# Layer 1's table split by batch, its preparation overlapped with gathers, and layer 2's mixing weights computed in layer 0

## The chip, the cores and the metric

The program runs on one core of one Trainium2 chip, in one launch. The core has five engines that run side by side and are held together by semaphores: PE (matrix multiply), DVE (vector), ACT (scalar), POOL (GpSimd) and SP, which here only issues DMAs. DMAs are issued from SP's queue or from POOL's, and share 16 DMA engines. The metric is the device time of one execution, in microseconds (us).

## The reference

Four layers on x of shape (2, 64, 64, 128): two batches of 4096 tokens with 128 channels. Layer 0 adds a selective scan, layer 1 a deformable convolution, layers 2 and 3 attention-like and feed-forward parts. The change touches layer 1, the beginning of layer 0, and a small preparation for layer 2. Layer 1, on the group-normed x:

```python
offsets = conv3x3(x, offset_w) + offset_b            # 18 = 9 taps x (dy, dx)
py = row + ky + dy;  px = col + kx + dx
y0, x0 = floor(py), floor(px);  wy, wx = py - y0, px - x0
val = gather(y0, x0)     * (1-wy)*(1-wx) + gather(y0, x0+1)     * (1-wy)*wx \
    + gather(y0+1, x0)   * wy*(1-wx)     + gather(y0+1, x0+1)   * wy*wx      # 0 outside the image
out = einsum('bhwkc,kcf->bhwf', val, kernel) + bias
x = x + out
```

Layer 2's feed-forward part mixes four sets of spectral filter matrices with weights from a softmax; the mixed matrices depend on weights alone, not on x:

```python
w = y_hard - y_soft + y_soft          # 4 weights
s = sigma ** 0.25                     # 16 filters
# for each of 4 segments: sums of w[i] * s[f] * (M_phi_plus[i, f] +- M_phi_minus[i, f]), and of w[i] * M_u[i]
```

## The kernel before

The kernel is written in a tile framework: the code lists instructions, and the framework orders them on each engine by a schedule of its own, places tiles in pools, and adds the waits. Pools lie on a stack: a pool that is opened after another has been closed takes its memory. Only inside `manual_schedule` (layer 0's scan loop and layer 2) is the order that of the code. X, the tokens of both batches (64 tiles of 128 tokens x 128 channels), stays on chip through layers 0 and 1.

The stages, in the order of the code (L1356 to L1400):

- X is loaded in 8 DMAs on SP (L1353). `zero_table` (L430) writes zeros over the whole table of layer 1 in DRAM with one DMA from POOL's queue (L437). The table has, for each batch, 67 x 67 cells of 4 x 128 floats (2 KB): cell (y, x) holds the four neighbours that bilinear sampling at that place needs.
- Layer 0 (L159). For each batch: transposes of X to channels (L95), group norm (L126: statistics, two small matmuls with `gmat`, then one pass over `xt`, L146), the gate `z` (L209 to L212, stored to DRAM from SP), the input projection (L221) and the depthwise convolution as 144 matmuls (L227), whose outputs ACT turns into U (L228). Then the scan over 32 chunks (L243 to L395; its first POOL instruction is L281), then the output part (L400 to L425). U and Y are tiles of a pool that lives through both batches (L189, L190).
- Layer 1 (L440), in two stages with pools of their own. Preparation, for batch 0 and then batch 1: transposes, group norm, a copy into the padded image `xp` (POOL, L466), transposes back into `xk` (L472), eight DMAs on SP that write `xk` into the table, shifted four ways (L480), the offset convolution as 72 matmuls with 18 weight columns each (L486; a float32 matmul leaves two records), transposes of the offsets (L491). After both batches: the index and weight arithmetic on DVE, for all 64 tiles at once (L507 to L524), into `idx` and `wt`. Then the loop over 64 tiles: nine gathers on POOL's queue (L534, 128 rows of 2 KB each) into G (three buffers), one multiplication on DVE into V (L541, two buffers), 36 matmuls against the identity that add the four corners and transpose (L553), three copies on ACT (L554), nine matmuls with the kernel (L557), one that adds the bias (L558), and an addition to X on DVE (L559).
- `mixing_weights` (L582) opens its pools before layer 1's, and `work()` is called after layer 1, so that its instructions run beside it: a few small operations, then for each of 16 filters two loads (L646, L647), arithmetic on DVE (L635, L637, L650, L652, L653) and a store (L654).
- `norm_tokens` (L564) takes the statistics of each of the 64 tiles of X (L571, L572), then `rs` and `sh` (L574), which layer 2's first normalisation reads (L729). X is stored to DRAM (L1387 by way of L1353).
- Layers 2 and 3, which the change does not touch.

Of the kernel before, what the change touches and what calls it, by code (L numbers as in the profile page):

```python
# [16 lines left out]
F32 = mybir.dt.float32  # L17
# [141 lines left out]
def layer0(k):  # L159
# [3 lines left out]
    with ExitStack() as es:  # L163
# [26 lines left out]
        Y = big.tile([P, 2, L], F32, name="Y")  # L190
        zs = dr.tile([2, P, B * L], F32, name="zs")

        for b in range(B):
            Xb = X[:, b * NTB : (b + 1) * NTB, :]
            with ExitStack() as e2:
# [20 lines left out]
                for h in range(2):  # L216
# [6 lines left out]
                    for q in range(8):  # L223
                        pc = ps.tile([P, N], F32, name="pc", tag="ps")
                        for t in range(9):
                            ky, kx = divmod(t, 3)
                            nc.tensor.matmul(pc, dw[:, h * 9 + t, :], xp[:, 8 * q + ky : 8 * q + ky + 8, kx : kx + WW], start=t == 0, stop=t == 8)  # L227
                        nc.scalar.activation(U[:, h, q * N : (q + 1) * N], pc, AF.Silu, bias=k.v("conv_b")[:, h : h + 1])  # L228

# [167 lines left out]
            with ExitStack() as e2:  # L397
                wk = e2.enter_context(tc.tile_pool(name=f"l0f{b}", bufs=2))
                ps = e2.enter_context(tc.tile_pool(name=f"l0fs{b}", bufs=6, space=PSUM))
                for q in range(8):  # L400
# [24 lines left out]
                    nc.vector.tensor_tensor(o, po.rearrange("p (a c) -> p a c", c=C), o, ALU.add)  # L425

# [3 lines left out]
def zero_table(k, pool, table):  # L430

    nc = k.nc
    row = B * TS * 4
    z = pool.tile([P, row], F32, name="zero")
    nc.gpsimd.memset(z, 0.0)
    flat = table.rearrange("a c -> (a c)").rearrange("(p g f) -> p g f", p=P, f=row)
    nc.gpsimd.dma_start(out=flat, in_=z.unsqueeze(1).to_broadcast([P, TS, row]))  # L437


def layer1(k, table):  # L440
    tc, nc, ins, X = k.tc, k.nc, k.ins, k.X
    with ExitStack() as es:
        enter = es.enter_context
        cst = enter(tc.tile_pool(name="l1c", bufs=1))
        wt = cst.tile([P, NT * 9, 4], F32, name="wt")
        idx = cst.tile([P, NT * 9], I32, name="idx")
        w_k = cst.tile([P, 9, C], F32, name="w_k")
        nc.sync.dma_start(out=w_k, in_=ins["kern1"].rearrange("t c f -> c t f"))

        with ExitStack() as e2:  # L450
            pre = e2.enter_context(tc.tile_pool(name="l1p", bufs=1))
            ps = e2.enter_context(tc.tile_pool(name="l1ps", bufs=6, space=PSUM))
            gmat = pre.tile([P, P], F32, name="gmat1")
            nc.sync.dma_start(out=gmat, in_=ins["gmat"])
            w_o = pre.tile([P, 9, 18], F32, name="w_o")
            nc.sync.dma_start(out=w_o, in_=ins["offw1"].rearrange("t c f -> c t f"))
            base = pre.tile([P, 2, NT, 9], F32, name="base")
            nc.sync.dma_start(out=base, in_=ins["base"])
            off = pre.tile([P, NT, 18], F32, name="off")
            for b in range(B):  # L460
                xt = pre.tile([P, L], F32, name="xt1")
                to_channels(k, ps, xt, lambda i: X[:, b * NTB + i, :], NTB)
                xp = pre.tile([P, 66, 66], F32, name="xp1", bufs=2)
                zero_frame(nc, xp)
                groupnorm(k, pre, ps, gmat, xt, "gn1")
                nc.gpsimd.tensor_copy(xp[:, 1:65, 1:65], xt.rearrange("p (h w) -> p h w", w=WW))  # L466

                xk = pre.tile([P, NTB, C], F32, name="xk")
                for g in range(0, NTB, 4):
                    pt = ps.tile([P, N], F32, name="pt1", tag="ps")  # L470
                    for j in range(4):
                        nc.tensor.transpose(pt[:, j * P : (j + 1) * P], xt[:, (g + j) * P : (g + j + 1) * P], k.ident)  # L472
                    k.copy(xk[:, g : g + 4, :].rearrange("p a c -> p (a c)"), pt)
                cells = table[b * TS * TS : (b + 1) * TS * TS, :].rearrange("(y x) c -> y x c", x=TS)
                for j in range(4):
                    dy, dx = divmod(j, 2)
                    for yy in range(2):
                        y0 = 2 - dy + yy
                        dst = cells[y0 : y0 + 63 : 2, 2 - dx : 66 - dx, j * C : (j + 1) * C]
                        nc.sync.dma_start(out=dst.rearrange("t x c -> x t c"), in_=xk[64 * yy : 64 * yy + 64, :, :])  # L480
                ot = pre.tile([18, L], F32, name="ot1")
                for q in range(8):
                    po = ps.tile([P, N], F32, name="po1", tag="ps")
                    for t in range(9):
                        ky, kx = divmod(t, 3)
                        nc.tensor.matmul(po[:18, :], w_o[:, t, :], xp[:, 8 * q + ky : 8 * q + ky + 8, kx : kx + WW], start=t == 0, stop=t == 8)  # L486
                    k.copy(ot[:, q * N : (q + 1) * N], po[:18, :])
                for g in range(0, NTB, 16):
                    pt = ps.tile([P, N], F32, name="pt2", tag="ps")
                    for j in range(16):  # L490
                        nc.tensor.transpose(pt[:, j * 18 : (j + 1) * 18], ot[:, (g + j) * P : (g + j + 1) * P], k.ident[:18, :18])  # L491
                    nc.vector.tensor_tensor(
                        off[:, b * NTB + g : b * NTB + g + 16, :],
                        pt[:, : 16 * 18].rearrange("p (a o) -> p a o", o=18),
                        k.r("offset_b").unsqueeze(1).to_broadcast([P, 16, 18]),
                        ALU.add,
                    )

            cell = pre.tile([P, 2, NT, 9], F32, name="cell")
            frac = pre.tile([P, 2, NT, 9], F32, name="frac")  # L500
            rest = pre.tile([P, 2, NT, 9], F32, name="rest")
            pt = pre.tile([P, NT, 9], F32, name="point")
            ti = pre.tile([P, NT, 9], I32, name="ti")
            tf = pre.tile([P, NT, 9], F32, name="tf")
# [11 lines left out]
            for b in range(B):  # L516
                s = slice(b * NTB, (b + 1) * NTB)
                nc.vector.tensor_scalar(cell[:, 0, s], cell[:, 0, s], float(TS), float((b * TS + 2) * TS + 2), ALU.mult, ALU.add)
            nc.vector.tensor_tensor(tf, cell[:, 0], cell[:, 1], ALU.add)
            nc.vector.tensor_copy(idx, tf.rearrange("p t o -> p (t o)"))  # L520
            for j in range(4):
                wy = (frac if j // 2 else rest)[:, 0]
                wx = (frac if j % 2 else rest)[:, 1]
                nc.vector.tensor_tensor(wt[:, :, j], wy.rearrange("p t o -> p (t o)"), wx.rearrange("p t o -> p (t o)"), ALU.mult)  # L524

        with ExitStack() as e2:
            gp = e2.enter_context(tc.tile_pool(name="l1g", bufs=3))
            wk = e2.enter_context(tc.tile_pool(name="l1w", bufs=2))
            ps = e2.enter_context(tc.tile_pool(name="l1gs", bufs=6, space=PSUM))
            po_ = e2.enter_context(tc.tile_pool(name="l1go", bufs=2, space=PSUM))  # L530
            for t in range(NT):
                G = gp.tile([P, 9, 4 * C], F32, name="G")
                for o in range(9):
                    nc.gpsimd.indirect_dma_start(  # L534
                        out=G[:, o, :],
                        out_offset=None,
                        in_=table,
                        in_offset=bass.IndirectOffsetOnAxis(ap=idx[:, t * 9 + o : t * 9 + o + 1], axis=0),
                    )
                V = wk.tile([P, 36, C], F32, name="V")  # L540
                nc.vector.tensor_tensor(  # L541
                    V,
                    G.rearrange("p o (q c) -> p (o q) c", c=C),
                    wt[:, t * 9 : (t + 1) * 9, :].rearrange("p o q -> p (o q)").unsqueeze(2).to_broadcast([P, 36, C]),
                    ALU.mult,
                )

                vt = wk.tile([P, 9 * P], F32, name="vt")
                for g, n in ((0, 4), (4, 4), (8, 1)):
                    pv = ps.tile([P, N], F32, name="pv1", tag="ps")  # L550
                    for o in range(n):
                        for q in range(4):
                            nc.tensor.matmul(pv[:, o * P : (o + 1) * P], V[:, (g + o) * 4 + q, :], k.ident, start=q == 0, stop=q == 3)  # L553
                    nc.scalar.copy(vt[:, g * P : (g + n) * P], pv[:, : n * P])  # L554
                po = po_.tile([P, C], F32, name="po2")
                for o in range(9):
                    nc.tensor.matmul(po, vt[:, o * P : (o + 1) * P], w_k[:, o, :], start=o == 0, stop=False)  # L557
# [18 lines left out]

DW = 257


def mixing_weights(k, dr, es):  # L582

# [918 lines left out]
```

## Time and profile before

| | us |
|---|---|
| median of 3 runs | 16111.0 |
| the runs | 16098.64 to 16113.83 |
| the profiled execution | 16122.4 |
| its span, from the first to the last instruction | 16120.6 |

Where the edits fall, in the profiled execution, in us from the span's start:

| stage | from | to |
|---|---|---|
| X loaded, table zeroed | 1.7 | 60 |
| layer 0, batch 0, up to the first POOL instruction of the scan (L281) | 60 | 227.66 |
| layer 0, the rest | 227.66 | 4673 |
| layer 1, preparation | 4673 | 4873.77 |
| layer 1, gathers, first start to last end | 4873.77 | 5851.14 |
| last V, last matmuls, statistics (to the start of L729) | 5853.98 | 5873.06 |
| layers 2 and 3 | 5873 | 16120.6 |

An engine's row in the profile gives the line of code, the operation, the tiles written and read, and the duration; text in brackets is how long the engine was idle before it, and what ended that. The granted clock is the share of full speed that PE's clock was given. DMA shares are means over the 16 DMA engines.

### The profile page before, as it was taken

How to read it: one execution, taken by the hardware profiler on the slowest of the kernel's cores; microseconds unless marked ns; L12 is line 12 of the kernel's file. 1: busy time of each engine (PE TensorE's matmuls, PEld its weight loads, DVE VectorE, ACT ScalarE, POOL GpSimd, SP SyncE). 2: the span in 40 equal slices, each digit the busy share in tenths (PEclk: the TensorE clock that was granted, in tenths of full speed). 3: DMA queues.
4: the chain of work that ended last, by engine and by line, in shares of the span. 5: the costliest groups of instructions: out<-in, count | busy, mean ns of one | idle time of the engine just before them, and what ended most of it. 6: DMA issues, size and time to landing. Idle time of an engine off the chain costs nothing.

```text
span 16120.6 us, 190989 instructions
## 1 busy us (share of the span) xinstructions
PE 12236.8 (76%) x69886; PEld 7246.4 (45%) x69886; DVE 13783.2 (86%) x12003; ACT 9835.0 (61%) x15912; POOL 13463.0 (84%) x5125
## 2 busy tenths in 40 slices
PE   6666657666667864549778679879788888888897
PEld 2222223222227851325445446546445555555565
DVE  4999975999964359999999999999999999999973
ACT  3666634666610027777777677777777777777752
POOL 3888835888817879999999999999999999999970
PEclk8999989999988876769889889989999999999998
DMA  2111111111135544546555556556666665565543
GB/s 102 69 71 69 68 51 49 70 71 69 69 93 160 160 143 151 168 150 203 183 187 195 174 181 199 193 184 203 192 193 198 189 204 195 190 205 194 188 169 128
DMA packets 1214859, 2389.69 MB, mean 148 GB/s; under 512 B 346648, under 2 KB 923288, under 8 KB 1047904
## 3 DMA queue, kind: packets, MB, share of 16 engines
q1 hardware_dynamic: 1162672, 2206.74, 41.7%
q0 software_dynamic: 50384, 169.42, 3.5%
q8 instruction: 552, 9.04, 0.2%
q14 instruction: 387, 3.17, 0.1%
q10 hardware_dynamic: 864, 1.32, 0.0%
HBM read 2018.49 MB, written 358.65 MB: 147 GB/s over the span
## 4 chain that ended last, share of the span: by engine, by line
POOL 34%; PE 13%; DVE 10%; DMA 3%; ACT 2%; issue 1%; SPq 0%; POOLq 0%; ACTq 0%; DVEq 0%
POOL S L1082 33%; DVE S L1138 10%; PE pef L966 6%; PE Z L1100 2%; PE acc L939 2%; DMA row<-drow 2%; PE pw L765 1%; POOL S L1088 1%; ACT ze L1106 1%; ACT dA L1136 0%; DMA w<-in_w_b_dram 0%; DMA w<-in_w_delta_dram 0%; ACT e L946 0%; PE acc L1001 0%; DMA e<-mdr 0%
## 5 line engine op out<-in xcount | busy, mean ns | idle before, releaser
L1138 DVE TENSOR_TENSOR_SCAN S<-dA,S 128x512 f32<-128x512 f32 x8192 | 9226.5, 1200 | 393.0 <-ACT dA L1136 208.4
L1082 POOL TENSOR_TENSOR S<-row,g 128x4096 f32<-128x4096 f32 x1024 | 9103.0, 8895 | 256.3 <-DMA row<-drow 219.8
L1136 ACT ACTIVATE dA<-row,a_t 128x512 f32<-128x512 f32 x8192 | 5614.4, 692 | 2146.0 <-DVE S L1138 2107.7
L1100 PE MATMUL Z<-S,cv 128*32 128x256 f32 x32768 | 2499.4, 435 | 1494.0 <-ACT ze L1106 1240.3
L966 PE MATMUL pef<-hk,ur 128*128 128x256 f32 x14336 | 3512.1, 388 | 138.8 <-ACT e L946 120.0
L966 PEld LDWEIGHTS pef<-hk,ur 128*128 128x128 f32 x14336 | 2644.6, 191 | 1077.6 <-issue 563.4
L365 DVE TENSOR_TENSOR_SCAN S<-dA,S 128x1024 f32<-128x1024 f32 x1024 | 2339.1, 2284 | 243.7 <-ACT dA L363 96.8
L354 POOL TENSOR_TENSOR S<-du,br 128x1024 f32<-128x1024 f32 x1024 | 2410.3, 2357 | 138.6 <-DVE M L379 83.3
L1100 PEld LDWEIGHTS Z<-S,cv 128*32 128x32 f32 x32768 | 999.9, 121 | 2698.6 <-issue 1289.2
L394 PE MATMUL yp<-M,ident 128*128 128x512 f32 x4096 | 2062.6, 627 | 2.9 <-DVE M L379 2.9
L394 PEld LDWEIGHTS yp<-M,ident 128*128 128x128 f32 x4096 | 821.7, 201 | 2091.7 <-issue 2052.7
L363 ACT ACTIVATE dA<-dt,an 128x511 f32<-128x511 f32 x2048 | 1406.9, 687 | 209.0 <-DVE S L365 132.0
L379 DVE TENSOR_TENSOR M<-S,pcn 128x1024 f32<-128x1024 f32 x1024 | 1250.5, 1221 | 110.5 <-DVE S L365 6.9
L323 PE MATMUL pcn<-cs,sel 80*128 80x512 bf16 x1024 | 409.3, 400 | 1180.4 <-DVE M L379 1169.8
L1106 ACT COPY ze<-Z 128x512 f32<-128x512 f32 x1024 | 1122.4, 1096 | 235.0 <-PE Z L1100 201.2
L939 PE MATMUL acc<-e,mw 128*128 128x512 f32 x1920 | 1042.2, 631 | 29.1 <-ACT e L946 28.5
L534 POOL DMA_INDIRECT G<-table,idx x576 | 802.2, 1393 | 261.1 <-issue 175.1
L966 PEld LDWEIGHTS pef<-hd,ur 128*128 128x128 f32 x4096 | 761.4, 195 | 491.7 <-issue 233.0
L966 PE MATMUL pef<-hd,ur 128*128 128x256 f32 (+1 forms) x4096 | 882.0, 342 | 99.8 <-ACT e L946 93.8
L541 DVE TENSOR_TENSOR V<-G,wt 128x4608 f32<-128x4608 f32 x64 | 317.5, 4962 | 609.0 <-DMA G<-table,idx 590.9
L367 ACT COPY stt<-S 128x2 f32<-128x2 f32 x896 | 168.9, 189 | 1083.5 <-DVE S L365 1080.3
L553 PE MATMUL pv<-ident,V 128*128 128x128 f32 x4608 | 615.3, 302 | 52.1 <-issue 48.8
(323 smaller groups left out, 8302.1 us busy)
## 6 DMA issues: line engine op xcount, KB each, us to landing
row<-drow SPq DMA_DIRECT2D x1024, 1024.0 KB
br<-bc SPq DMA_DIRECT2D x256, 1024.0 KB
zd<-ze SPq DMA_DIRECT2D x1024, 256.0 KB
hk<-in_phi_dram SPq DMA_DIRECT2D x128, 576.5 KB
hk<-in_phi_dram SPq DMA_DIRECT2D x96, 704.5 KB
hd<-in_phi_dram SPq DMA_DIRECT2D x512, 128.5 KB
mw<-wdr SPq DMA_DIRECT2D x480, 128.0 KB
hk<-in_phi_dram SPq DMA_DIRECT2D x160, 320.5 KB
```

The source lines that it names most:

```text
L354: nc.gpsimd.tensor_tensor(S, du, br[:, n % 4, :].unsqueeze(1).to_broadcast([P, 2, T]), ALU.mult)
L363: nc.scalar.activation(dA[:, h, rest], dt[:, h, rest], AF.Exp, scale=an[:, kk * 2 + h, n : n + 1])
L365: nc.vector.tensor_tensor_scan(flat, dflat, flat, 0.0, ALU.mult, ALU.add)
L379: nc.vector.tensor_tensor(M, S, pcn.unsqueeze(1).to_broadcast([P, 2, T]), ALU.mult)
L394: nc.tensor.matmul(yp[:, h, :], k.ident, M[:, h, :], start=False, stop=n == 15)
L939: nc.tensor.matmul(acc.rearrange("p a s -> p (a s)"), ms[f][:, o, :], e, start=box["first"], stop="whole" in box and (f, o) == todo[-1])
L966: nc.tensor.matmul(pe[:, a, 256 - n :], ur[:, par, j, :], h[:, at : at + n], start=i == 0, stop=i + 1 == len(mm))
L1082: nc.gpsimd.tensor_tensor(S, row.unsqueeze(1).to_broadcast([P, 2, R, T]), g.unsqueeze(2).to_broadcast([P, 2, R, T]), ALU.mult)
L1100: nc.tensor.matmul(Z[32 * j : 32 * j + 32, q], cv[:, h, s], S[:, h, :, s], start=h == 0, stop=h == 1)
L1106: nc.scalar.copy(ze.rearrange("p q t e -> p q e t"), Z)
L1136: nc.scalar.activation(dA, row[:, j % R, :], AF.Exp, scale=a_t[:, h, d : d + 1])
L1138: nc.vector.tensor_tensor_scan(s, dA, s, 0.0, ALU.mult, ALU.add)
```

## The change

Four things are done, in layer 0, layer 1 and the zeroing of the table:

- The table becomes two tables, one for each batch, and only the cells at the border are zeroed (two double rows at top and bottom, and a strip of four cells across each row's end), in six DMAs on POOL's queue.
- Layer 1 has one set of pools. Each batch has its own `idx` and `wt`, and its own index arithmetic, at half the width. The loop of gathers over all 64 tiles follows. Its preparation pool has one buffer a tile. G has four buffers, and V is written in place in G. The copy to `xp` is made on ACT. The bias is added to X ahead of the loop, on DVE, for a whole batch at once, and its matmul is left out.
- The offset convolution has weights padded to 32 columns; four matmuls, for four row groups of the image, write to four column groups of PE and four partition groups of one PSUM tile, so that two such tiles hold a batch's offsets. They are turned back with four full transposes each.
- `mixing_weights` is split into its DRAM tiles and `work(es)`, and layer 0 calls `work` at the end of batch 0's preparation, with pools inside that stage's. Y moves to a pool of its own for each batch, opened after that stage.

```diff
-def layer0(k):
+def layer0(k, mix=None):
...
-        Y = big.tile([P, 2, L], F32, name="Y")
...
+                if b == 0 and mix is not None:
+                    mix(e2)
+
+            yb = es.enter_context(ExitStack())
+            Y = yb.enter_context(tc.tile_pool(name=f"l0y{b}", bufs=1)).tile([P, 2, L], F32, name="Y")
...
+            yb.close()
...
 def zero_table(k, pool, table):
-    row = B * TS * 4
-    z = pool.tile([P, row], F32, name="zero")
+    z = pool.tile([P, 4 * 4 * C], F32, name="zero")
     nc.gpsimd.memset(z, 0.0)
-    flat = table.rearrange("a c -> (a c)").rearrange("(p g f) -> p g f", p=P, f=row)
-    nc.gpsimd.dma_start(out=flat, in_=z.unsqueeze(1).to_broadcast([P, TS, row]))
+    cell = 4 * C
+    for b in range(B):
+        flat = table[b].rearrange("a c -> (a c)")
+        for y in (0, TS - 2):
+            rows = flat[y * TS * cell : (y + 2) * TS * cell].rearrange("(p f) -> p f", p=P)
+            nc.gpsimd.dma_start(out=rows, in_=z[:, : 2 * TS * cell // P])
+        edge = flat[(TS + TS - 2) * cell :]
+        dst = bass.AP(edge.tensor, edge.offset, [[TS * cell, TS - 3], [1, 4 * cell]])
+        nc.gpsimd.dma_start(out=dst, in_=z[: TS - 3, :])
...
 def layer1(k, table):
...
+        pre = enter(tc.tile_pool(name="l1p", bufs=1))
+        gp = enter(tc.tile_pool(name="l1g", bufs=4))
+        wk = enter(tc.tile_pool(name="l1w", bufs=2))
+        ps = enter(tc.tile_pool(name="l1ps", bufs=3, space=PSUM))
+        gs = enter(tc.tile_pool(name="l1gs", bufs=3, space=PSUM))
+        po_ = enter(tc.tile_pool(name="l1go", bufs=2, space=PSUM))
...
+        w_o = cst.tile([P, 9, 32], F32, name="w_o")
+        nc.vector.memset(w_o, 0.0)
+        nc.sync.dma_start(out=w_o[:, :, :18], in_=ins["offw1"].rearrange("t c f -> c t f"))
+        wts, idxs = [], []
+        for b in range(B):
...
+            nc.vector.tensor_tensor(Xb, Xb, k.r("bias1").unsqueeze(1).to_broadcast([P, NTB, C]), ALU.add)
...
-                nc.gpsimd.tensor_copy(xp[:, 1:65, 1:65], xt.rearrange("p (h w) -> p h w", w=WW))
+            nc.scalar.copy(xp[:, 1:65, 1:65], xt.rearrange("p (h w) -> p h w", w=WW))
...
+            for g in range(2):
+                po = ps.tile([P, N], F32, name="po1", tag="ps")
+                for t in range(9):
+                    ky, kx = divmod(t, 3)
                     for j in range(4):
-                        nc.tensor.matmul(po[:18, :], w_o[:, t, :], xp[:, 8 * q + ky : 8 * q + ky + 8, kx : kx + WW], start=t == 0, stop=t == 8)
-                    k.copy(ot[:, q * N : (q + 1) * N], po[:18, :])
...
+                        q = 4 * g + j
+                        nc.tensor.matmul(po[32 * j : 32 * j + 32, :], w_o[:, t, :], xp[:, 8 * q + ky : 8 * q + ky + 8, kx : kx + WW], start=t == 0, stop=t == 8)
+                ot = pre.tile([P, N], F32, name="ot1", bufs=2)
+                k.copy(ot, po)
...
+            idx = cst.tile([P, NTB * 9], I32, name=f"idx{b}")
...
+        for t in range(NT):
+            b, i = divmod(t, NTB)
...
+                    in_=table[b],
...
+            V = G.rearrange("p o (q c) -> p (o q) c", c=C)
+            nc.vector.tensor_tensor(V, V, wts[b][:, i * 9 : (i + 1) * 9, :].rearrange("p o q -> p (o q)").unsqueeze(2).to_broadcast([P, 36, C]), ALU.mult)
...
-                nc.tensor.matmul(po, k.ones, k.r("bias1")[0:1, :], start=False, stop=True)
...
-def mixing_weights(k, dr, es):
+def mixing_weights(k, dr):
...
+    def work(es):
+        cst = es.enter_context(tc.tile_pool(name="f2c", bufs=1))
+        wp = es.enter_context(tc.tile_pool(name="f2w", bufs=2))
...
-                    table = dr.tile([B * TS * TS, 4 * C], F32, name="table")
+                    table = [dr.tile([TS * TS, 4 * C], F32, name=f"table{b}") for b in range(B)]
...
+                    weights, mix = mixing_weights(k, dr)
                 if "0" in stages:
-                    layer0(k)
...
+                    layer0(k, mix)
...
+                if "1" in stages:
+                    layer1(k, table)
...
```

## The prediction

> **What bounds the kernel now.** I read the page first, then the busy time by stretches, then the timeline of the two stages that the edits touch, then the waits. The groups of the page put most of the time into layer 2 (scan L1138 on DVE, inputs L1082 on POOL), which no edit touches. What can move is layer 0 up to its scan and layer 1, which runs from 4673 to 5873 us.
>
> The stretches show two plain bounds. Columns: stretch, its length, busy time of PE, weight loads, DVE, ACT, POOL, then granted clock, share of the DMA engines, GB/s.
>
> ```profile
> 45.00:50.00 5.00, 0.00 (x0) 0.00 (x0) 0.00 (x0) 0.00 (x0) 0.00 (x0) 0.50 1.04 413
> 100.00:150.00 50.00, 50.00 (x118) 22.08 (x117) 0.00 (x0) 4.81 (x7) 0.00 (x0) 1.00 0.00 0
> 4725.00:4730.00 5.00, 5.00 (x13) 1.17 (x12) 0.00 (x0) 0.07 (x1) 0.00 (x0) 1.00 1.00 219
> 5420.00:5470.00 50.00, 44.17 (x336) 42.49 (x336) 16.91 (x12) 4.61 (x10) 40.56 (x31) 0.90 0.57 162
> ```
>
> At 45 us every engine is idle and the DMA engines are full: the table's zeros. From 100 us layer 0's convolution fills PE while DMA and DVE do nothing. At 4725 us PE (offset convolution, L486) and DMA (table writes, L480) are both full. In the gathers nothing is full, though POOL comes near. The timeline there (start, length, engine, line) says why:
>
> ```profile
> 5397.24 4.96 DVE L541 TENSOR_TENSOR V<-G,wt 128x4608 f32<-128x4608 f32 x1 [10.72 <-DMA G<-table,idx]
> 5398.24 4.79 POOL L534 DMA_INDIRECT G<-table,idx  x1 [0.30 <-issue]
> 5402.12 0.28 DVE L559 TENSOR_TENSOR X<-po,X 128x128 f32<-128x128 f32 x1
> 5402.44 0.29 DVE L571 BATCH_NORM_STATS2 st<-X 128x6 f32<-128x128 f32 x1
> 5402.77 0.18 DVE L572 BATCH_NORM_AGGREGATE mv<-st 128x2 f32<-128x6 f32 x1
> 5403.34 0.95 POOL L534 DMA_INDIRECT G<-table,idx  x1 [0.30 <-issue]
> ```
>
> Eight gathers of a tile take 0.96 us each, 0.30 apart. The one caught by DVE's run takes 4.79 and ends 0.08 us after L572, the last operation of that run (5402.95 to 5403.03). I checked all 64 tiles: each has one long gather, and from the fourth on it ends 0.08 or 0.09 after L572. So POOL sets the pace: 9 x 1.26 + 3.8 = 15.1 us a tile, and 977.4 us from the first gather (4873.77) to the end of the last (5851.14). V waits for gathers 590.9 of its 609.0 idle us; PE has slack (12.7 of 15.1).
>
> The waits give the two ends of the stages:
>
> ```profile
> PE pm L136 <- DMA gmat<-in_gmat_dram: 25.5, 1, 25.5
> DVE ot L72 <- PE po L486: 79.4, 6, 14.8
> ACT rt L625 <- PE po L423: 12.2, 1, 12.2
> ```
>
> Layer 0's group norm waits 25.5 us for a 64 KB matrix that is queued behind the zeros. Layer 1's offsets wait for the convolution. The third line I use for memory: `rt` is 64 bytes at the bottom of the new pools, and it waited for the last matmul of layer 0, not for the tile that had lain there: a pool's memory comes free when the pools before it are done.
>
> **Zeros in border cells.** Before: 18.4 MB (17,956 KB, L437). After: per batch two double rows of 2 x 67 x 2 KB and 64 x 8 KB, 1.06 MB; 2.1 MB in all. 16.3 MB less at 413 GB/s = 39.4 us by which gmat, and everything behind it up to the scan, comes earlier (the sum pm starts at 62.97 now). Bounds: 35 (X's 4.2 MB, in rows of 512 bytes, at the 294 GB/s that like loads reach at 4680 us) to 43 (gmat right behind X). I take **-39**. Six short POOL issues take the place of one of 3.2 us; POOL is idle there until 227 us.
>
> **Mixing weights in layer 0.** All of L602 to L654 moves: 16 rounds of L635 0.344, three L637 of 0.478, L650 0.746, L652 0.684, L653 0.682 = 3.89 us, 62 us of DVE; 32 loads and 16 stores on SP, with mu and mdr 18.3 MB: 62 us at 294 GB/s, 85 at the 216 of the table writes. What hides it is the convolution L227, 92 to 223 us, with DVE busy 2.8 us of 100 and DMA at zero. Started behind gmat at about 24 us it ends near 150; the scan would start at about 185 (223 less 39). It is queued on SP among the 16 zs stores (L212, 16.9 us); z waits for these ten times already, 3.1 us in all, and behind z stand PSUM and PE. Bounds 0 to 17 (that stretch doubled); I take **+6**, nearer the 3.1. Two table loads on ACT (1.28 each) fall where ACT idles. If the cover were gone see the rivals. Y, now below the scan's pools, is first written after the convolution either way: 0.
>
> **Batch 0's preparation.** Now the first gather waits for both batches: two convolutions of 62 us one after the other (288 records, 123.9 us busy), and the index work at double width. After, it needs only table 0 and idx 0. Table: writes start at 4700.65 now. The bias add on X (128x4096, 4.96 x 4096/4608 = 4.4 us) comes ahead of part of the group norm; the mix's operations between its steps go, 1.5 us; the copy to xp goes from POOL (3.9 us) to ACT, by its rows 8 x 0.59 = 4.7 at most, ahead of ACT's half of the xk copies, some 3 us. So xk is full at about 4706; 8.4 MB at 218 GB/s = 38.5 us; landed at 4745, gathers from 4747. Offsets: four column tiles side by side. Z at L1100 is the like: 2499.4 us for 32,768 records of 256 columns, 76 ns each, against 123.9/288/2 = 215 for L486. So 144 records of 512 columns take 22 us, not 62; with copies, transposes and index work at half width (8 us) idx 0 is there near 4735, before the table. DVE's queue may hold batch 1's xk copies, which wait for xk to be written out, ahead of idx 0: up to 15 us. I take half of that doubt, gathers from 4752: **-122**. Bounds: -130, and -101 if the column tiles run one at a time (idx at 4772).
>
> **The loop.** Batch 1's 8 MB of table writes and its PE and DVE work now lie beside batch 0's gathers. DMA: 8.4 MB ask for 38 us of full engines beside a loop that uses 0.55, some 85 us of crowding; four G buffers hold 60 us of issue against a life of about 40 (issue 15, landing 3, V 5, PE 13), so landings may slip 20 us before POOL feels it: 0. PE: two times 32 transposes and 22 us more against 2.4 us of slack a tile: absorbed in a dozen tiles. DVE: xt and xk copies 5.5, bias 4.4, statistics 5.0, small ones 1.6, normalising 2.4, offsets 1.6, index work 8: 28.5 us, each of which holds a gather up. Bounds 0 to 29; about half runs before 4752, I take **+12**. G now lives until PE has read it, the in-place V takes as long as before.
>
> L571 and L572 leave the loop: their pool now lies where w_k is, and so waits for the last po. Each tile's DVE run ends 0.55 earlier (5402.40 for 5402.95): 63 x 0.55 = **-35**, with POOL at 14.7 us a tile and PE at 12.
>
> [...] Here the rows show the end of the gather after L572 in 61 tiles, and I go by them.
>
> **The tail.** The same 64 pairs come after the last po: 0.42 us from a pair's start to the next operation (5859.18 to 5859.60), 63 x 0.42 = 26.5 us, ahead of sh (L574) and of layer 2's first xn (L729, released by sh at 5873.06). The bias matmuls (L558) go: 0.8 us of this. **+26**. Bounds 0 (the pool lies elsewhere; then the 35 are not gained either) to 32.
>
> **Sum.** -39 + 6 - 122 + 12 - 35 + 26 = -152. The profiled execution took 16122.4 us (span 16120.6), so 15970; it lay 11 above the runs' median of 16111.0, so the forecast is **15,960 us**. Layers 2 and 3 are unchanged; the runs spread over 15 us.
>
> **Rivals.** (a) The mix keeps its old pace: 4676.65 to 4917 is 240 us; from 24 it would end at 264, and the scan's pools, which take its memory, wait 79 us for it: less the 6, 16,033. For: the release shown by `rt`, two buffers a round, an SP queue that waits. Against: the old pace came from 16 MB of table writes and a busy DVE. 12%.
> (b) The start is held: column tiles one at a time, idx 0 behind batch 1's work, PE 40 us late once more: 21 + 25 more, 16,006. 13%.
> (c) The change doesn't overlap: something of batch 1 (POOL's frame, DVE's order) stands before batch 0's gathers, which then start when table 1 is written, near 4795: 43 - 12 more, 15,991. 7%.
> (d) Slower: the mix is queued behind the convolution, whose outputs end at 184, and runs for its 240 us before the scan: 240 - 6 more, 16,194. It decides from an end of the mix later than about 184 + 158 + 32 = 374 us. For: it is called after the convolution. Against: it was called last before as well, and its first load left 4 us after layer 1 began. 8%.
> My case has 60%.
>
> **How the numbers follow.** My own case reaches from 15,915 (all best bounds: -43, -130, -35, +26, less spread) to 16,000. With (b), (c) and most of (a), and the costs at their upper ends together, I give 15,910 to 16,045. About 0.2% (32 us) is what a measurement here can tell from no change; below 16,079 lie my case, (b), (c) and most of (a): 87%. Within: 5%. Above: 8%.
>
> **What would show it.** pm at 22 to 28 us, the scan's first POOL operation (L281, now 227.66) near 195; the last wdr store before that. First gather 4752 less about 33, long gathers near 4.2 us, ending after the X add; 64 bn pairs in a row after the last po; L1's column tiles overlapping as L1100 does. Wrong if wdr stores run up to the scan's start, if gathers wait for buffers, or if POOL's long gathers multiply in batch 0's half by more than 29 us in sum.

## The result, and the profile after

The changed kernel takes **15,975.8 us** (median of 4 runs, 15,964.0 to 15,978.7); the kernel before, run beside it, 16,112.4 (4 runs, 16,098.6 to 16,122.8). The ratio is 0.9914, with a 95% interval from 0.9897 to 0.9932: some 137 us or 0.9% less. The profiled execution has a span of 15,975.1 us, for 16,120.6 before: 145.5 us less. Cut at the same events in both traces, these go as follows (us; the columns "before" and "after" are times between the two events).

| stretch | before | after | measured | forecast |
|---|---|---|---|---|
| start to group norm's first product, pm | 62.97 | 25.24 | -37.7 | -39 |
| pm to the first z product, pz | 6.2 | 16.9 | +10.7 | +6 for the mix in layer 0 |
| pz to the scan's first POOL operation (L281, now L285) | 158.5 | 159.0 | +0.5 | in the same +6 |
| rest of layer 0 | | | -2.2 | 0 |
| start of layer 1 to the first gather | 200.9 | 72.9 | -128.0 | -122 |
| first gather to the end of the last | 977.4 | 969.3 | -8.1 | +12 - 35 = -23 |
| last gather to layer 2's first xn | 21.9 | 44.9 | +23.0 | +26 |
| layers 2 and 3 | 10247.5 | 10243.9 | -3.6 | 0 |
| sum | | | -145.5 | -152 |

The size of the whole is as forecast; two of its terms are not: the loop's, and the time between pm and the scan. Both are seen in the timeline (start, length, engine, line, operation, and in brackets the idle time before it and what ended it). The rows set at 0, layers 2 and 3 and the rest of layer 0, move by as much between profiles of code that is the same there: layers 2 and 3 take 10,238.7 to 10,249.3 us in seven profiles of the changed kernel and its variants, and from the scan's first POOL operation to the first gather it is 4511.5 to 4517.4 us in seven.

Layer 0's start, kernel after:

```profile
25.24 0.56 PE L136 MATMUL pm<-gn_mv,gmat 128*128 128x1 f32 x2 [7.22 <-DMA gmat<-in_gmat_dram]
...
30.05 0.42 DVE L649 TENSOR_SCALAR mus<-mu,w 128x384 f32<-128x384 f32 x1 [2.17 <-DMA mu<-in_mu_dram]
...
32.26 3.65 DVE L177 CAST sel<-ident 16x2048 bf16<-16x2048 f32 x3
...
37.63 0.15 DVE L84 TENSOR_TENSOR gn_s<-gn_rs 128x1 f32<-128x1 f32 x1
...
42.12 8.05 PE L208 MATMUL pz<-xt,w_in 128*128 128x512 f32 x12 [14.63 <-DVE xt L146]
```

The zeros' part came as forecast: pm waits for gmat until 25.2. But between two small steps of the same group norm DVE now waits for mu, the mix's first load (L649), and then makes layer 0's constants (L175 to L187, 6.4 us); before, those ran at 92 to 99 us, beside the convolution. L84 could have run at about 30.5 and runs at 37.6, and xt, which the products of z wait for, is late with it.

The start of layer 1, kernel after (SPq is SP's DMA queue; the length of the table writes is that of their issue):

```profile
4650.94 4.42 DVE L479 TENSOR_TENSOR X<-X,rv 128x4096 f32<-128x4096 f32 x1
...
4671.09 7.93 PE L506 MATMUL po<-xp,w_o 128*32 128x512 f32 x72
...
4671.81 35.97 SPq L497 DMA_DIRECT2D table<-xk  x8
...
4705.75 0.29 DVE L541 CAST idx<-tf 128x288 int32<-128x288 f32 x1
4716.97 1.07 POOL L554 DMA_INDIRECT G<-table,idx  x1 [27.92 <-DMA base<-in_base_dram]
```

The column-tiled convolution of a batch is two such rows of 72 products, 15.9 us for the 62 before. The index table idx is ready at 4706.0, the first gather starts at 4717.0: the table comes last, as forecast. (The row names the load of `base` for batch 1, which stands on SP's queue right behind the table's eight writes. In a later profile of the same kernel the last write lands at 4710.43, `base` at 4711.19, and the first gather starts at 4711.40, so some 0.8 us of the wait are that load's.)

The loop, kernel after, the same stretch of a tile that the prediction showed of before:

```profile
4808.77 4.96 DVE L561 TENSOR_TENSOR G<-G,wt 128x4608 f32<-128x4608 f32 x1 [9.73 <-issue]
4809.97 4.58 POOL L554 DMA_INDIRECT G<-table,idx  x1 [0.30 <-issue]
4813.65 0.28 DVE L573 TENSOR_TENSOR X<-po,X 128x128 f32<-128x128 f32 x1
4814.86 0.94 POOL L554 DMA_INDIRECT G<-table,idx  x1 [0.30 <-issue]
```

L585 and L586 (L571 and L572 before) have left the loop, and yet the long gather is no shorter: 4.87 us on average (63 of them) for 4.86. It ends at 4814.55, 0.82 us after V's end (4813.73). All 63 do, within 0.01, and read again so do those of before: V at 5397.24 + 4.96 ends at 5402.20, the gather at 5403.03, 0.83 later. The profile of before had two tiles that tell the readings apart, the first two held gathers of its loop, where no L571 and L572 stand behind V, but the mix:

```profile
4893.40 4.96 DVE L541 TENSOR_TENSOR V<-G,wt 128x4608 f32<-128x4608 f32 x1 [10.71 <-DMA G<-table,idx]
4894.50 4.68 POOL L534 DMA_INDIRECT G<-table,idx  x1 [0.30 <-issue]
4898.27 0.68 DVE L652 TENSOR_TENSOR wf<-smf 128x512 f32<-128x512 f32 x1
4898.87 0.69 DVE L653 TENSOR_TENSOR wf<-smf 128x512 f32<-128x512 f32 x1
4899.48 1.00 DVE L637 SCALAR_TENSOR_TENSOR smf<-m,w,smf 128x256 f32<-128x256 f32 x2
```

DVE's run goes on until 4900.48; the gather ends at 4899.18, 0.82 after V.

The tail, kernel after:

```profile
5711.74 0.29 DVE L573 TENSOR_TENSOR X<-po,X 128x128 f32<-128x128 f32 x1 [9.76 <-PE po L572]
5711.95 0.48 DVE L585 BATCH_NORM_STATS2 st<-X 128x6 f32<-128x128 f32 x2
...
5728.70 0.20 DVE L81 TENSOR_SCALAR ln_v<-mv 128x64 f32<-128x64 f32 x1
```

Sixty-four pairs stand behind the last po: 16.7 us, 0.26 each. A further 6.7 us come from PE, which ends 17.5 us after the last V (5694.2 to 5711.7) and not 10.8 as before; in the other profiles with this loop it is 12.6 to 16.9.

### The profile page after: what moved, and what is told of

Same layout as the page of the kernel before. It is cut to its first block, busy times and chain, and to the rows that moved or that the text cites. A ratio compares the mean times of both kernels' runs of the same rounds, so it can differ in the third digit from the quotient of the medians.

```text
span 15975.1 us, 190775 instructions
## 1 busy us (share of the span) xinstructions
PE 12073.9 (76%) x69710; PEld 7165.8 (45%) x69710; DVE 13769.0 (86%) x12022; ACT 9836.5 (62%) x15906; POOL 13444.5 (84%) x5128
## 4 chain that ended last, share of the span: by engine, by line
POOL 38%; PE 17%; DVE 16%; issue 4%; ACT 3%; DMA 3%; another core or an unknown queue 2%; SPq 0%; POOLq 0%; DVEq 0%; ACTq 0%
POOL S L1095 35%; DVE S L1151 9%; PE pef L979 6%; DVE S L369 5%; PE Z L1113 2%; PE pv L568 2%; PE acc L952 2%; DMA row<-drow 2%; PE yp L398 1%; DVE M L383 1%; PE pw L778 1%; PE po L572 1%; POOL S L358 1%; POOL S L1101 1%
## 5 line engine op out<-in xcount | busy, mean ns | idle before, releaser
L561 DVE TENSOR_TENSOR G<-G,wt 128x4608 f32<-128x4608 f32 x64 | 317.5, 4961 | 626.4 <-DMA G<-table,idx 546.1
L959 ACT COPY e<-pef 128x512 f32<-128x512 f32 x960 | 557.9, 587 | 110.4 <-PE pef L979 61.4
## 6 DMA issues: line engine op xcount, KB each, us to landing
mw<-wdr SPq DMA_DIRECT2D x480, 128.0 KB
```

## The experiments

Theory: V alone, and none of the short operations behind it, holds the gather; the other late term is DVE's order. All experiments start from the changed kernel. Where a single run's time is compared, it has some 15 us of spread (14.8 between the changed kernel's four runs), so the steps are read from events of the trace.

**The statistics back in the loop.** The pool of L585/L586 is opened ahead of layer 1's, so that it waits for nothing.

```diff
-def norm_tokens(k, rs, sh):
+def norm_tokens(k, pre, rs, sh):
...
-                if "1" in stages:
-                    layer1(k, table)
-                if two:
-                    norm_tokens(k, rs, sh)
+                with tc.tile_pool(name="l2n", bufs=1) as stp:
+                    if "1" in stages:
+                        layer1(k, table)
+                    if two:
+                        norm_tokens(k, stp, rs, sh)
```

> The statistics' pool is opened ahead of layer 1, so the 64 pairs L585/L586 run inside the loop again, one behind each X add. Theory A (what the changed kernel's rows suggest: a long gather ends 0.82 us after the end of V, whatever follows V): the loop keeps 15.15 us a tile (969 us), long gathers keep 4.87; behind the last po one pair is left in place of 64, so 62 x 0.26 = 16 us less: 15,960. Rival B (the prediction's reading: any DVE operation of the run holds the gather): long gathers grow by 0.55, loop +35 us, tail -16: 15,995.

Measured: 15,962.9 us (4 runs). The pairs run behind each X add, the loop takes 967.3 us (965 to 970 in every run that leaves V and the column tiles as changed), long gathers 4.86, every one ending 0.81 to 0.82 after V. From the last gather to xn 28.1 us for 44.9. Theory A; the 35 us of B are nowhere.

```profile
5666.67 4.96 DVE L561 TENSOR_TENSOR G<-G,wt 128x4608 f32<-128x4608 f32 x1 [9.56 <-DMA G<-table,idx]
5671.55 0.28 DVE L573 TENSOR_TENSOR X<-po,X 128x128 f32<-128x128 f32 x1
5671.87 0.29 DVE L585 BATCH_NORM_STATS2 st<-X 128x6 f32<-128x128 f32 x1
5672.19 0.18 DVE L586 BATCH_NORM_AGGREGATE mv<-st 128x2 f32<-128x6 f32 x1
```

**V's second operand out of SBUF.** V keeps its length and work; its weights are read from PSUM. To make room there, `po` has one buffer in place of two.

```diff
-        po_ = enter(tc.tile_pool(name="l1go", bufs=2, space=PSUM))
+        po_ = enter(tc.tile_pool(name="l1go", bufs=1, space=PSUM))
+        pw_ = enter(tc.tile_pool(name="l1wp", bufs=1, space=PSUM))
...
+            wp = pw_.tile([P, 36], F32, name="wp")
+            nc.vector.tensor_copy(wp, wts[b][:, i * 9 : (i + 1) * 9, :].rearrange("p o q -> p (o q)"))
-            nc.vector.tensor_tensor(V, V, wts[b][:, i * 9 : (i + 1) * 9, :].rearrange("p o q -> p (o q)").unsqueeze(2).to_broadcast([P, 36, C]), ALU.mult)
+            nc.vector.tensor_tensor(V, V, wp.unsqueeze(2).to_broadcast([P, 36, C]), ALU.mult)
```

> A tile's 36 weights are copied to PSUM on DVE (about 0.2 us) and V reads them there, so V has one SBUF input and one PSUM input and still takes about 5 us. Theory A (it is V's second SBUF input that keeps POOL from its descriptors): no long gathers, POOL needs 9 x 1.25 = 11.3 us a tile, PE 12.7 becomes the bound: loop 720 to 815 us in place of 969, kernel 15,730 to 15,830. Rival B (any long DVE operation holds a gather, whatever its inputs): long gathers stay at 4.9, the loop grows by at most 64 x 0.2, kernel 15,976 to 15,990.

Measured: 15,956.6 us (4 runs, 15,954.0 to 15,983.7), so half a hit. No gather is long any more: 949 ns on average. But POOL gained only 24 us, since it now waited for PE to free G (group of the gathers: busy, mean ns, then idle time and what ended it):

```profile
L555 POOL DMA_INDIRECT G<-table,idx x575 | 545.8, 949 | 398.8 <-PE pv L571 234.7 <-issue 163.4 <-DVE wp L563 0.3
```

PE took 14.8 us a tile, with pauses of mostly 0.4 to 1.7 us between products that wait for nothing in the trace (of 146.7 us of idle time ahead of the products of L571, 141.9 are put down to issue). Two more runs ask what that is.

**Half of PE's sums.** On top of the edit before; two of the four corners are left out of the sum.

```diff
-                    for q in range(4):
-                        nc.tensor.matmul(pv[:, o * P : (o + 1) * P], V[:, (g + o) * 4 + q, :], k.ident, start=q == 0, stop=q == 3)
+                    for q in range(2):
+                        nc.tensor.matmul(pv[:, o * P : (o + 1) * P], V[:, (g + o) * 4 + q, :], k.ident, start=q == 0, stop=q == 1)
```

> V's weights in PSUM, and PE sums only two of the four corner products of each tap (36 transposing products per tile become 18; two corners are left out of the result). Theory A (with the hold gone PE sets the pace, at 14.8 us a tile, where the trace shows 12.2 busy and 2.2 idle with nothing to wait for): POOL's 11.3 us a tile is next, loop 722 to 760 us in place of 946, kernel 15,735 to 15,770. Rival B (the landing of the gathers or the four G buffers set the 14.8): the loop stays near 946, 15,956.

Measured: 15,723.2 us (one run), some 12 below A's range; gathers and gaps 11.25 us a tile. Theory A in kind: POOL could go at that pace, and neither the landing of the gathers nor the number of G buffers hinders it. It doesn't tell why PE was slow, nor that the halved sums were needed: it ran in another session.

**The same kernel again.**

> The kernel with V's weights in PSUM, once more. Its loop took 946 us in place of 720 to 815, with PE issuing one product every 0.7 us or a multiple while DMA was busy, though it waited for nothing that the trace shows; the same loop with three further edits took about 11.3 us a tile. Theory A (the slow issue belongs to that execution of the program, not to the code: PE's loop is instruction for instruction the same in both): 15,735 to 15,790 this time. Rival B (it belongs to the code, through one of the three other edits): 15,956 again.

Measured: **15,738.9 us** (4 runs, 15,729.4 to 15,742.9; ratio to before 0.9763, interval 0.9747 to 0.978). Here each tile takes 11.25 us and the loop 722.8. V and the gathers beside it:

```profile
5206.74 0.94 POOL L555 DMA_INDIRECT G<-table,idx  x1 [0.30 <-issue]
5206.90 4.95 DVE L564 TENSOR_TENSOR G<-G,wp 128x4608 f32<-128x4608 f32 x1 [6.08 <-DMA G<-table,idx]
5207.98 0.95 POOL L555 DMA_INDIRECT G<-table,idx  x1 [0.30 <-issue]
5209.23 0.94 POOL L555 DMA_INDIRECT G<-table,idx  x1 [0.30 <-issue]
```

V takes 4.95 us as ever (4.96 with both operands in SBUF), and the gathers beside it 0.95, for 4.87. So the hold goes here with V's second SBUF operand; neither V's length nor its engine makes it. The slow PE is not in the code alone: the same kernel shows it in the trace of one session (runs taken together; a loop of 946 us) and not in the next one's (722.8), and by their times all four runs of the first have it and none of the next. The two sessions ran on different chips, so what belongs to a session can't be told here from what belongs to a chip. The first session's row of windows (stretch, its length, busy time of PE with the number of products, weight loads, DVE, ACT, POOL, granted clock, DMA share, GB/s):

```profile
5205.00:5209.00 4.00, 3.66 (x32) 3.50 (x31) 0.00 (x0) 0.59 (x1) 3.08 (x4) 1.00 0.76 212
5209.00:5213.00 4.00, 1.58 (x10) 1.38 (x10) 0.00 (x0) 0.40 (x1) 1.18 (x2) 1.00 0.64 186
5213.00:5217.00 4.00, 4.00 (x23) 4.00 (x22) 3.58 (x1) 0.35 (x2) 2.85 (x3) 0.57 0.40 111
```

In the second row PE issues 10 products where 38 fit (so many are issued from 5217 to 5221, at clock 1.00), and in the third it runs at a little over half the clock.

**DVE's order in layer 0.** The constants (sel and dd, now made from `late`) and the mix are made to depend on the normalised xt.

```diff
+                if b == 0:
+                    nc.vector.scalar_tensor_tensor(late, xt[:, :P], 0.0, k.ident, ALU.mult, ALU.add)
...
+                    for i in range(8):
+                        nc.vector.tensor_scalar(dd[:, i, :], late, k.v("ds")[:, i : i + 1], None, ALU.mult)
...
+        nc.vector.scalar_tensor_tensor(w4, late[:, 0:4], 0.0, w4, ALU.mult, ALU.add)
```

> In layer 0 the selection matrix, the D diagonals and the mixing weights' first products are made to depend on batch 0's normalised xt (a copy of the identity to which 0 times xt is added), so none of them can stand between the small steps of the group norm. Theory A (the 10.7 us between pm and the first pz are DVE's order): pz 6 to 7 us after pm as in the kernel before, layer 0's first scan operation L285's like near 191 in place of 201, kernel 15,965. Rival B (SP's queue, the DMA traffic of the mix or PE sets that start): the scan starts at 201 again, 15,976.

Measured: 15,965.3 us (4 runs); pm 25.46, pz 32.84 (7.4 us for 16.9), the scan's first POOL operation at 192.65 for 201.07. Theory A, 8.4 us of it; other profiles that leave this start as changed have 15.3 to 15.9 for the 16.9 and the scan at 199.9 to 200.5, so 7 to 8 us is as much as is sure.

**All zeros again**, in two transfers of 9.2 MB.

> All 18.4 MB of the two tables are zeroed again, in two transfers; the rest as changed. Theory A (the 37.7 us by which the group norm's first product pm came earlier are the zeros' bytes): pm near 63 us again; the mix's DVE work and the constants find DVE idle or not as before, so the start of the scan moves by 28 to 38 us: 16,003 to 16,013. Rival B (X and the constants' loads set pm): 15,976.

Measured: 16,026.3 us (one run); pm at 54.11, not 63, the scan's first operation at 253.23, 52.2 later than with the change. A's direction, but the step is larger than its range, and the trace says why:

```profile
57.33 0.15 DVE L85 TENSOR_TENSOR gn_s<-gn_s,gn_v 128x1 f32<-128x1 f32 x1
82.87 0.42 DVE L642 TENSOR_SCALAR mus<-mu,w 128x384 f32<-128x384 f32 x1 [25.39 <-DMA mu<-in_mu_dram]
83.21 0.15 DVE L86 TENSOR_SCALAR gn_s<-gn_s 128x1 f32<-128x1 f32 x1
```

The mix's first operation stands in DVE's queue between L85 and L86 of the group norm and waits 25.4 us for mu, whose load lies behind the zeros. The mix in layer 0 costs little only because the zeros are gone. Of the 37.7 us at pm, 28.9 went back, and the run is not the kernel before over again: POOL issues the second transfer at 47.23 only, and gmat, behind X's loads on SP, leaves at 48.20 (56.13 before, 20.23 with the change). So only the first 9.2 MB lie ahead of pm, and they go at 230 to 290 GB/s, for 413 before; the other half of the zeros lies ahead of mu. That the zeros' bytes set pm is shown, the price of all of them at 413 GB/s is not.

**The mix behind layer 1.**

```diff
-                    layer0(k, mix)
+                    layer0(k)
...
                     layer1(k, table)
                 if two:
+                    with ExitStack() as e2:
+                        mix(e2)
```

> The mixing weights are made behind layer 1, in memory that lies on layer 1's, beside nothing; the rest as changed. In layer 0 they took 93 us from the first load (22.9) to the last store (116). Theory A (hidden altogether in layer 0, save for DVE's order): 75 to 95 us more behind layer 1, some 9 us back in layer 0, so 16,040 to 16,065. Rival B (the prediction's rival: they keep the 240 us which they took beside the table writes): 16,200.

Measured: 16,034.6 us (one run), 5 under A's range. The mix alone takes 69 us from its first load of m (5696.0) to its last store (5765.2), and in layer 0 it took 93 (22.9 to 116.0), beside the group norm, the products of z and the first part of the convolution (65.7 to 196). pz comes 12.9 us after pm here, with the constants alone between L84 and L85: so of the 10.7 us they are the larger part (6.4) and the mix's own operations the rest.

**One table for both batches.**

```diff
-            nc.vector.tensor_scalar(cell[:, 0], cell[:, 0], float(TS), float(2 * TS + 2), ALU.mult, ALU.add)
+            nc.vector.tensor_scalar(cell[:, 0], cell[:, 0], float(TS), float((b * TS + 2) * TS + 2), ALU.mult, ALU.add)
...
-                    table = [dr.tile([TS * TS, 4 * C], F32, name=f"table{b}") for b in range(B)]
+                    both = dr.tile([B * TS * TS, 4 * C], F32, name="table")
+                    table = [both[b * TS * TS : (b + 1) * TS * TS, :] for b in range(B)] + [both]
...
-                    in_=table[b],
+                    in_=table[B],
```

> Both batches' cells lie in one tensor again and the gathers read that tensor, so batch 0's gathers wait for batch 1's writes too (last issued at 4764.8). Theory A (the split into two tables is what starts the gathers early; batch 1's work costs the loop next to nothing): first gather about 55 us later, loop 2 us shorter at most, 16,015 to 16,035. Rival B (batch 1's preparation beside the gathers costs the loop about 12 us, as predicted): first gather as late, loop 12 shorter, about 16,018 with long gathers shorter in the first tiles. Rival C (the split is not what releases the gathers): 15,976.

Measured: 16,023.2 us (one run), first gather at 4764.9 (48 later; counted from layer 1's start 125.2 us for 72.9, so 52), loop 970.0. Theory A: the loop without batch 1's work beside it isn't shorter than with it (969.3, and 965.2 to 967.7 in other profiles), so that work costs next to nothing.

**One product at a time in the offset convolution.**

```diff
-                    for j in range(4):
-                        q = 4 * g + j
-                        nc.tensor.matmul(po[32 * j : 32 * j + 32, :], w_o[:, t, :], xp[:, 8 * q + ky : 8 * q + ky + 8, kx : kx + WW], start=t == 0, stop=t == 8)
+                    nc.tensor.matmul(po[:18, :], w_o[:, t, :18], xp[:, 8 * q + ky : 8 * q + ky + 8, kx : kx + WW], start=t == 0, stop=t == 8)
```

> Layer 1's offset convolution with its 18 columns, one product after the other, as before; the rest as changed. Theory A (the column tiles are needed too: 16 us for a batch become 62, and the indices then come later than the table): first gather 30 to 40 us later, at about 4750, 16,005 to 16,015. Rival B (the table's writes, which end at 4716, set the start alone): 15,976.

Measured: 16,071.0 us (one run), 95 more and over twice what A said. The first gather starts at 4758.1, 41 later, about as A has it, and waits for idx now. What A left out is batch 1's convolution, beside the gathers: nine products of it at 7.90 us a row stand in PE's queue between the tiles, and POOL waits twice for G, 62.5 us in all.

```profile
4758.12 1.10 POOL L552 DMA_INDIRECT G<-table,idx  x1 [16.28 <-DVE idx L539]
...
4846.37 0.94 POOL L552 DMA_INDIRECT G<-table,idx  x1 [29.36 <-PE pv L566]
```

**The changed kernel again**, as a yardstick.

> The changed kernel as it is, on the same chip and between the same runs of the kernel before as the others of this call: 15,965 to 15,985. It is there so that steps of 10 to 20 us can be read.

Measured: 15,973.1 us (5 runs, 15,960.2 to 15,985.3), ratio 0.9912. In this profile the tail is 40.0 us, for 44.9, and PE ends 12.6 us after the last V, for 17.5: its lateness is not the same each time.

**All edits together**: the statistics early, V's weights in PSUM, layer 0's constants and mix late, and the bias added to X behind a batch's index work.

> The three edits of the earlier runs together (statistics' pool open ahead of layer 1, V's weights in PSUM, layer 0's constants and mixing weights behind the group norm), and the addition of the bias to X moved behind a batch's index work, so that it doesn't stand before the first table's group norm (4.42 us). If the parts add up: tail -17, loop -24, layer 0 -8, first gather -4, together 53 us under the changed kernel: 15,922. If PE, which sets the pace of the loop once no gather is held, takes back what the others give (bn pairs cost it nothing, so this could only be the later start of a PE already full): 15,935.

Measured: **15,713.6 us** (5 runs, 15,703.5 to 15,719.7), ratio 0.9747 (0.9734 to 0.976), far under both expectations, which had taken the slow PE's loop for the kernel's. The loop takes 725.3 us, PE's granted clock in it is 0.97 for 0.89; the tail is 34.0. The first gather starts at 4710 for 4717, but counted from layer 1's start it is at 72.8 us, as in the changed kernel (72.9): the gain is layer 0's. The addition of the bias did not move on DVE. It stands behind the index work in the code (L550), and the framework's schedule still puts it between two steps of the group norm:

```profile
4644.36 3.65 DVE L132 BATCH_NORM_STATS2 gn_st<-xt 128x6 f32<-128x512 f32 x6
4647.93 4.41 DVE L550 TENSOR_TENSOR X<-X,rv 128x4096 f32<-128x4096 f32 x1
4652.25 0.36 DVE L133 BATCH_NORM_AGGREGATE gn_mv<-gn_st 128x2 f32<-128x48 f32 x1
```

> The version with all edits, once more and on the same chip as the run before this one. If the slow issue belongs to the execution it may show here as well: 15,920 then, 15,714 without.

Measured: 15,707.8 us (4 runs, 15,705.4 to 15,717.4), ratio 0.9747 (0.9731 to 0.9763). No slow PE in either profile of this version, nor by the times of its nine runs.

## Why the prediction held, and where it didn't

The forecast was 15,960 us, the time is 15,976. The sum missed by 6.5 us; the rest is that the profiled execution before lay 11 above the median and the one after does not. Step by step:

- **Zeros, -39: right in size**, 37.7 at pm, and the zeros do set it. The price, bytes over the rate of the stretch where DMA alone was busy, fits; the run with all zeros again, whose transfers went at a lower rate (230 to 290 GB/s for 413), doesn't test it.
- **The mix, +6: right that it hides, wrong in what it costs.** The price was 11.2 us (9 to 10 in other profiles), inside the bounds of 0 to 17. The prediction put it on SP's queue and the z stores; pz to the scan moved by 0.5 us. It was DVE's order, between pm and pz; 7 to 8 us of it went when that order was changed. The prediction had the clue and used it for layer 1 only, where it counted 1.5 us for "the mix's operations between its steps"; it did not carry the same thought along to the place where the mix goes. Nor did it ask what else runs in the idle time that a shorter wait leaves: the constants were before at 92 us.
- **Batch 0's start, -122: right**, 128.0. The table is the last wait (but for the 0.8 us of `base` behind it), none of the 15 us of doubt about batch 1's copies was needed, and the column tiles overlap as the rows of L1100 said (15.9 us for an estimate of 22). Undone, the two tables cost 52 us at the first gather and the column tiles 42, both counted from layer 1's start, so each is needed; the column tiles are needed a second time, in the loop, which took 55 us more without them (1024.3 for 969.3), where the prediction's rival (b) had 25.
- **Batch 1's work, +12: near nothing.** Beside its DVE work three gathers took more than 1.0 us, 1.13 on average, and POOL waited once for G, 1.3 us: some 2 us in all, close to the prediction's lower bound of 0. Its reason was wrong with the next term's: not every operation of DVE holds a gather. The bias addition, the long one with two SBUF inputs, was over at 4699.2, before the first gather.
- **L571 and L572 leave the loop, -35: wrong, and this is the step that failed.** They left it, and the held gathers stayed at 4.87 us; put back, they stayed at 4.86. The prediction read "ends 0.08 us after L572" in 61 tiles as cause. L559, L571 and L572 followed V at a constant distance of 0.75 us, so any of the four ends would have fitted; 61 tiles of the same pattern are one observation. The two tiles that could decide, with the mix's operations behind V, were among the three that it set aside by "from the fourth on": there the gather ends 0.82 and 0.83 after V, in the middle of DVE's run. The length of a gather without V beside it speaks for V's end too: 0.96, so that 0.82 after the release would be nearly the whole of its work. The 8.1 us that the loop did gain are the first gather (6.44 to 1.07 us) and shorter ordinary gathers (0.956 to 0.947 on average, 512 of them); why these are shorter no run tells.
- **The tail, +26: right**, 23.0, but of two parts: the pairs cost 0.26 each and not 0.42, since in a row they interleave (a next one starts every 0.26 us), and PE was 6.7 us later.

What of V holds the gather is shown by one pair: with two SBUF inputs 4.87 us for the gather, with one 0.95, though V is as long (4.96 and 4.95 us). Two SBUF inputs in a short operation cost little: beside two of L546 (two SBUF inputs, 0.7 us) gathers took 1.00 and 1.23 us. The first gather of the kernel before, 6.44 us beside a run of the mix's operations, stays unexplained. What the gather is doing while it is held no run here shows; the descriptors that the expectation for V's weights in PSUM speaks of were the author's guess.

So the 35 us that didn't come were met by terms that came out better than the sum had them: 10 of batch 1's work, 10 of the first and the ordinary gathers, 6 of the start, 3 of the tail, 6 in stretches set at 0, which is no more than they vary by, less 5 of the mix and 1 of the zeros; 6.5 us are left. That the total fits so well is therefore in part luck.

## What to carry to other kernels

When something ends a fixed time after the last operation of a run, look for a tile where the run is shorter or longer, or make one, before a price is put on that operation; here two such tiles lay at the loop's start. V, a vector operation with two SBUF inputs, held one gather that GpSimd issued for 3.9 us of its 5.0, in 63 of 64 tiles (4.87 us for 0.95); one operand in PSUM took that away, 237 us of the whole, where the change under study had gained 137. What is moved into a stretch "with an idle engine" joins that engine's queue where the schedule puts it, which need not be where the code has it: look for the short, dependent operations which it can land between, and for the load that it waits for.

## What the runs showed of the hardware

PE was slow without a wait that the trace shows: in one session of the kernel with weights in PSUM, products of the column tiles (7.93 us for 72 in other rows) came one by one while the DMA share was above 1.0 (1.10 from 4752 to 4756, with 2 products in these 4 us):

```profile
4752.11 1.01 PE L507 MATMUL po<-xp,w_o 128*32 128x512 f32 x1 [1.96 <-issue]
4754.91 1.01 PE L507 MATMUL po<-xp,w_o 128*32 128x512 f32 x1 [1.79 <-issue]
```

and in the next, with the DMA as full (1.09 from 4752 to 4756, with 40 products), all 72 together:

```profile
4744.50 9.71 PE L507 MATMUL po<-xp,w_o 128*32 128x512 f32 x72
```

The starts lie mostly 0.7 us or a multiple of it apart (2.80, 3.05, 3.50, 1.40, 2.10 and 1.41 from 4752.11 on), and in the loop's windows above PE pauses from 5205 to 5213, at DMA shares of 0.76 and 0.64, and is busy throughout from 5213 to 5217, at 0.40. It cost 218 us (15,956.6 for 15,738.9). The changed kernel has it too: batch 1's first row of 72, beside gathers and table writes, takes 21.1 us in its first profile and in those of two experiments of the slow session (the statistics, DVE's order), and 7.93 in every profile of the later sessions; with one table for both batches, so with no gathers beside it, it takes 7.93 in the slow session as well. What sets it off stays open: sessions ran on different chips, and no run tells them apart.

In the loop the clock's records show 1.00 or 0.50. After the loop's first 100 us the changed kernel, where PE idles for up to 5.6 us, has 43 stretches at 0.50, 32 of 3.41 us and 11 of 6.83, and a mean of 0.89; of the 34 in the whole loop of the kernel before, 32 take 6.83 or 10.24 us. The fast loops have two to four in the same part, PE idles for 2.9 us at most, and the clock is 0.99 on average (0.97 to 0.98 over the whole loop). A single long idle stretch is not needed for 0.50: the loop with the slow PE has 43 as well, at idle stretches of 1.7 us at most (0.89 from 4715 to 5660), and in its windows above PE is busy for 1.58 us of the 4 before 5213, at 1.00, and the mean is 0.57 in the next 4. What sets the clock to 0.50 no run shows.
